# Two hypernetwork convolutions on one core: 128-column weight products, tiles in groups of two, layer 2's x loaded by ScalarE

## The chip, the core and the metric

The kernel runs on one core of one Trainium2 chip. The metric is the time of one execution in microseconds (us); the time before is 4005.55 us, the median of three runs (4001.37 to 4008.61). All arithmetic is in fp32. The engines are TensorE (PE, with its weight loads PEld shown apart), VectorE (DVE), ScalarE (ACT), GpSimd (POOL), and SyncE (SP), which here only issues DMAs.

## The reference

Two equal layers follow each other. Each normalizes x by groups of positions, makes its own convolution weights for every sample and position from z, convolves, and adds a bias and x:

```
h = relu(ln(z @ W1 + b1, g1, be1))                      # z: (32, 256, 16) -> (32, 256, 128)
w = (h @ W2 + b2).reshape(B, L, CI, CO, K)              # 64*64*3 weights for each of 32*256 (b, l)
bias = (relu(ln(z @ Wb1 + bb1)) @ Wb2 + bb2).transpose(0, 2, 1)
x_uf = jnp.stack([xp[..., i:i + L] for i in range(K)], axis=-1)
out = jnp.einsum('sbilk,bliok->sbol', x_uf, w) + bias[None]
x = x + out(_gn(x))                                     # x: (32, 32, 64, 256), 32 groups of 8 positions
```

Most of the arithmetic is h @ W2: 8192 positions, each with 128 inputs and 12288 outputs, in each layer.

## The kernel before

**Units.** A layer is cut into 32 units (8 groups of four samples, 4 quarters of the positions), and each unit into two half-units of 32 output channels. There are 128 half-units, v = 0 to 127; the first 64 are layer 1. A half-unit has two parts on TensorE. First the *weight tiles*: 12 tiles of 8 output channels, made by `make` (L615) and moved to `wall` by `take` (L626). Then the *products* (L665): `wall` against the normalized x in `xn`, added to the residual in one of the three slots of `ring`.

**A weight tile.** W2 lies in `w2` as 128 x (64 channels x 192 columns), three blocks of 64 columns per channel. `make` writes one PSUM tile `pg` of 128 x 8 x 128. For each channel it has two products of 64 stationary columns and 128 moving ones, one for the lower and one for the upper half of the partitions (L622, L623). Kind 0 takes blocks 1 and 2 with the odd positions, kind 1 blocks 0 and 1 with the even ones, and kind 2 (the shared one) block 2 with the even and block 0 with the odd ones. For kinds 0 and 1 `take` is one VectorE addition of b2 over all partitions (L634). For kind 2 VectorE adds the lower 64 partitions and then ScalarE the upper 64, by eight activations (L645), whose first waits for VectorE's addition. `pg` comes from a pool of three buffers of two PSUM banks (`ps_g`); which of them a tile gets is decided while the program is built.

**Order.** The tiles of a half-unit come in the order kind 0, 2, 1, four times. The loop at L821 writes out half-unit v as: the matmuls of its first tile, then `products(v - 1)`, then `take` of the first tile and the other tiles; behind tile k it writes the work that `agenda(v)` lists for k. That covers storing the finished half-unit, loading the next residual and bias (`after`, L725), the normalization of the next half of a unit on GpSimd (`next_half`, L694) with the load of the half after it, the bias addition on GpSimd, and in layer 1 the statistics and the *rims*: `take_edges` copies the outer columns on ScalarE behind tile 1, `turn_edges` transposes them on TensorE behind tile 3. Every engine and DMA queue works through its own list in this order.

**Loads of x.** In layer 1 half a unit is one DMA (L168) of SP's queue. In layer 2 it is four DMAs of 32 partitions in short pieces (L177), also of SP's queue, into `raw` or `land`.

**The start.** `first_phase` (L440) streams x in 22 pieces for the statistics of the first groups (L458), runs the small hypernetworks and makes the first weight tiles. Behind piece 19 it normalizes unit 0 on VectorE (`starting`, L759); behind that stand the last two pieces. The bias of half-unit 0 is loaded into `xn` behind piece 18 and added behind piece 19.

Of the kernel before, what the change touches and what calls it, by code (L numbers as in the profile page):

```python
# [30 lines left out]
P = 128  # L31
K = 3
G = 32
NT = 4
# [9 lines left out]
def conv_layers(  # L44
# [78 lines left out]
    def place_of(u):  # L123
        n, r = divmod(u, UL)
        return (n, *divmod(r, BG))
# [37 lines left out]
    def load_half(u, k, buf=None):  # L163

        buf = raw if buf is None else buf
        n, q, bg = place_of(u)
        if n == 0:
            nc.sync.dma_start(out=by_slot(buf), in_=xp[u][:, k * NT // 2 : (k + 1) * NT // 2])  # L168
            return
        if k == 0:  # L170
            load_edges(u)
        for a in range(2):
            for h in range(NH):
                rows = slice((1 - a) * C + h * CH, (1 - a) * C + (h + 1) * CH)
                src = x1[u - UL][h][k * NT // 2 * S : (k + 1) * NT // 2 * S]
                src = src.rearrange("(t s) (o a m) -> a o t s m", s=S, a=2, m=MT)[a]
                nc.sync.dma_start(out=by_sample(buf)[rows, :, :, a : a + MT], in_=src)  # L177

    def residual(v):
        return ys[:, v % RING]  # L180
# [259 lines left out]
    def first_phase(first_weights, first_bias, add_bias, starting):  # L440
# [3 lines left out]
        needed = BG * (GT + 1) // LAND  # L444
        slots = [ring[:, k * LAND * GE : (k + 1) * LAND * GE] for k in range(RING)] + [land[:, 0 : LAND * GE]]
        slots = [s.rearrange("p (k x) -> p k x", k=LAND) for s in slots]
        order = [i % 4 for i in range(needed - 2)] + [0, 1, 2, 1, 2, 1]
        assert len(order) == units

        def load(i):  # L450
# [12 lines left out]
        with tc.tile_pool(name="stage", bufs=1) as stage:  # L463
# [33 lines left out]
            def batch(j):  # L497
                return made[j] if 0 <= j < count else None

            for i in range(units):  # L500
                j, odd = divmod(i, 2)
                if batch(j - 2):
                    for k in range(2 * odd, 2 * odd + 2):
                        batch(j - 2).bias(k)
                if odd:
                    if batch(j):
                        batch(j).variance()
                    if batch(j - 1):
                        batch(j - 1).hidden(0)
                        batch(j - 1).hidden(1)  # L510
                else:
                    if batch(j):
                        batch(j).form()
                    if batch(j - 1):
                        batch(j - 1).turn()
                if i == needed:
                    merge = Merge(first_parts.rearrange("p g b f -> p g (b f)")[:, 0 : GT + 1], 0, 0)
                    table = Table(0)
                    merge.sums()
                    merge.around()  # L520
                if i == needed + 1:
                    merge.mean()
                    add_bias(0)
                    merge.root()
                    table.expand(nc.vector)
                stats(i, range(2))
                if i == needed:
                    merge.spans()
                stats(i, range(2, LAND))
                if odd and batch(j):  # L530
                    batch(j).scale()
                if i == 3:
                    nets[1].prepare(stage)
                if i == 6:
                    for x in range(2):
                        load_hidden(x)
                if i == needed - 2:
                    load_half(0, 1, land)
                    load_residual(0)
                if i == needed - 1:  # L540
                    load_half(0, 0)
                    load_w2(0, CH, C)
                if i == needed:
                    first_bias()
                if i == needed + 1:
                    table.lay(table.spread(), [nc.vector.tensor_copy, nc.scalar.copy])
                    starting()
                first_weights(i - (needed - 11))
            load_residual(1)

    with tc.manual_schedule():
        bts = {}
# [62 lines left out]
        def make(h, kind, o0):  # L615
            pg = ps_g.tile([P, OG, M], FP, tag="pg", name="pg")
            even, odd = h[:, 0, :], h[:, 1, :]

            (k0, h0), (k1, h1) = (((1, odd), (2, odd)), ((0, even), (1, even)), ((2, even), (0, odd)))[kind]
            for k in range(OG):  # L620
                w = w2[:, o0 + k, :]
                nc.tensor.matmul(pg[0:C, k, :], w[:, k0 * C : (k0 + 1) * C], h0, start=True, stop=True)  # L622
                nc.tensor.matmul(pg[C:P, k, :], w[:, k1 * C : (k1 + 1) * C], h1, start=True, stop=True)  # L623
            return pg

        def take(pg, n, kind, o0):  # L626
# [64 lines left out]
        def place_half(u, k):  # L691
            return land if k == 1 and u >= 3 * BG else raw

        def next_half(u, k):  # L694

            if u >= U:
                return
            if k == 0 and u % BG == 0 and u // BG in tables:
                t = tables.pop(u // BG)
                t.lay(t.from_spot(), [nc.gpsimd.tensor_copy])  # L700
            normalize(u, k, place_half(u, k))
            u, k = (u, 1) if k == 0 else (u + 1, 0)
            if u < U:
                load_half(u, k, place_half(u, k))

        pieces = [(j, bg, g) for j in range(1, NQ) for g in range(FIRST[j]) for bg in range(BG)]
        base = BG * FIRST[0]
# [17 lines left out]
        def after(v):  # L725

            u, h = divmod(v, NH)
            store(v)
            load_pieces(v + 1)
            if v + 2 < NH * U:  # L730
                load_residual(v + 2)
                load_bias(v + 2)
            if h == 1 and u % 2 == 1 and u + 3 < U:
                load_hidden((u + 3) // 2)

        starts = range(0, CH, OG)
        order = [(kind, o) for o in starts for kind in (0, 2, 1)]

        def weights(v, k, between=None):
            u, h = divmod(v, NH)  # L740
# [25 lines left out]
                    normalize(0, k, bufs[k], nc.vector, j0, j1)  # L766
            load_half(1, 0)

        def first_bias():
            x = xn.rearrange("p n t j s -> p (n t j s)")  # L770
            h = x.shape[1] // 2
            load_bias(0, x[:, h : h + CH * LT].rearrange("p (o l) -> p o l", l=LT))

        first_phase(first_weights, first_bias, add_bias, starting)
        bp = ctx.enter_context(tc.tile_pool(name="bias", bufs=1))
        load_bias(1)
        normalize(1, 0)
        load_half(1, 1)
        add_bias(1)

        def agenda(v):

# [1 line left out]
            u, h = divmod(v - 1, NH)  # L784
            todo[0].append(lambda: last_stats(v - 1))
            todo[0].append(lambda: after(v - 1))
            todo[2].append(lambda: next_half(*((u + 1, 1) if h == 0 else (u + 2, 0))))
            if v + 1 < NH * U:
                todo[5].append(lambda: add_bias(v + 1))
            if v <= last_of[NQ - 1]:  # L790
# [24 lines left out]
            if v <= NH * UL:  # L815
                todo[1].append(lambda: take_edges(v - 1))
                if h == 1:
                    todo[3].append(lambda: turn_edges(u))
            return todo

        for v in range(1, NH * U):  # L821
# [101 lines left out]
```

## Time and profile before

| what | us |
|---|---|
| median of three runs | 4005.55 |
| the profiled execution | 4010.21 |
| its span, first to last instruction | 4008.4 |
| PE busy in the span | 3810.9 (95%) |
| DVE, ACT, POOL busy | 2592.2, 1285.8, 1939.5 |
| mean granted share of TensorE's clock | 0.986 |

The profile was taken in an execution of its own, which is 4.66 us above the median. Busy times are unions over an engine's instructions. TensorE's matmuls overlap (an fp32 product is two MATMUL rows), so its speed is read from the distances between starts.

### The profile page before, as it was taken

What the parts mean: (1) busy time and instruction counts of PE and PEld (TensorE: products, weight loads), DVE (VectorE), ACT (ScalarE), POOL (GpSimd) and SP (SyncE); (2) the same over time, 40 slices, a digit from 0 to 9 for tenths busy, and PEclk for the clock granted to TensorE, in tenths of its full rate; (3) what the DMA queues carried; (4) which work ended last, traced back from release to release, by engine and by line L of the source; (5) the groups of instructions that cost most, each with busy time, mean ns of one, the idle gap of its engine ahead of it and who ended that gap; (6) DMA issues with size and microseconds to landing.
All of it is one profiled execution on the core that took longest, in us unless ns stands there. A gap on an engine that the chain in (4) does not pass through costs nothing.

```text
span 4008.4 us, 185362 instructions
## 1 busy us (share of the span) xinstructions
PE 3810.9 (95%) x86548; PEld 3675.3 (92%) x86548; DVE 2592.2 (65%) x2954; ACT 1285.8 (32%) x4431; POOL 1939.5 (48%) x655
## 2 busy tenths in 40 slices
PE   6699999999999999999999999999999999999999
PEld 3499999999999999999989999999999999999998
DVE  4677777777777776666665555555555555555655
ACT  3423333323333333333323323323233233333332
POOL 2154445444544445544545545555546545645551
PEclk7799999999999999999999999999999999999999
DMA  8666556556556555445488878878788788788782
GB/s 271 233 201 195 180 177 193 177 172 195 177 178 196 173 168 159 134 153 156 134 196 154 148 132 160 145 147 151 140 166 141 140 156 141 147 150 140 157 146 87
DMA packets 644660, 657.76 MB, mean 164 GB/s; under 512 B 562600, under 2 KB 570160, under 8 KB 578096
## 3 DMA queue, kind: packets, MB, share of 16 engines
q1 hardware_dynamic: 624688, 633.30, 65.5%
q8 instruction: 677, 11.09, 1.2%
q10 hardware_dynamic: 19200, 12.59, 1.0%
q14 instruction: 95, 0.78, 0.1%
HBM read 496.91 MB, written 148.90 MB: 161 GB/s over the span
## 4 chain that ended last, share of the span: by engine, by line
PE 80%; DVE 6%; ACT 6%; issue 2%; DMA 1%; POOL 0%; SPq 0%; ACTq 0%; POOLq 0%; DVEq 0%
PE pg L622 49%; PE pc L676 24%; PE pg L623 6%; ACT wall L645 5%; DVE wall L634 4%; DMA bt<-bd 1%; DVE ring L685 1%; DVE parts L341 0%; POOL ring L566 0%; DVE xn L608 0%; PE pe L586 0%; DVE first_parts L723 0%; ACT rim L581 0%; PE over L371 0%; SPq L559 0%
## 5 line engine op out<-in xcount | busy, mean ns | idle before, releaser
L622 PE MATMUL pg<-hT,w2t 128*64 128x128 f32 x24576 | 2752.5, 274 | 26.7 <-issue 24.0
L623 PE MATMUL pg<-hT,w2t 128*64 128x128 f32 x24576 | 2753.3, 274 | 17.0 <-issue 16.7
L622 PEld LDWEIGHTS pg<-hT,w2t 128*64 128x64 f32 x24576 | 2689.0, 137 | 63.9 <-issue 37.9
L623 PEld LDWEIGHTS pg<-hT,w2t 128*64 128x64 f32 x24576 | 2689.2, 137 | 23.1 <-issue 22.7
L634 DVE TENSOR_TENSOR wall<-pg,b 128x1024 f32<-128x1024 f32 (+1 forms) x1536 | 1874.1, 1220 | 726.0 <-PE pg L623 720.1
L645 ACT ACTIVATE wall<-pg,b 64x128 f32<-64x128 f32 x4096 | 1158.8, 465 | 2596.1 <-DVE wall L634 2596.0
L566 POOL TENSOR_TENSOR ring<-ring,bt 128x2048 f32<-128x2048 f32 x127 | 578.1, 4552 | 1200.9 <-DMA bt<-bd 755.1
L676 PEld LDWEIGHTS pc<-wall,xn 128*32 128x32 f32 x36864 | 914.8, 110 | 110.3 <-issue 61.2
L676 PE MATMUL pc<-wall,xn 128*32 128x128 f32 (+1 forms) x36864 | 951.6, 262 | 64.1 <-issue 34.7
L685 DVE TENSOR_TENSOR ring<-pc,ring 128x512 f32<-128x512 f32 x512 | 353.9, 691 | 622.2 <-PE pc L676 617.9
L608 POOL TENSOR_TENSOR xn<-raw,tab 128x2112 f32<-128x2112 f32 x86 | 440.1, 5118 | 447.2 <-PE pc L676 433.7
L608 POOL TENSOR_TENSOR xn<-xn,tab 128x2112 f32<-128x2112 f32 x126 | 591.4, 4693 | 9.9
L608 POOL TENSOR_TENSOR xn<-land,tab 128x2112 f32<-128x2112 f32 x40 | 224.3, 5609 | 111.9 <-DMA land<-x 102.0
L341 DVE BATCH_NORM_STATS2 parts<-ring 128x6 f32<-128x256 f32 x512 | 192.1, 417 | 6.5
L723 DVE BATCH_NORM_STATS2 first_parts<-land 128x6 f32<-128x512 f32 x168 | 114.5, 681 | 0.6 <-DMA land<-in_xg_dram 0.6
L433 POOL COPY tab<-spot 64x1024 f32<-64x1024 f32 x28 | 29.0, 1035 | 94.1 <-ACT spot L420 93.2
L276 POOL TENSOR_TENSOR raw<-w2t,xn 128x256 f32<-128x256 f32 x16 | 10.3, 644 | 113.7 <-DVE xn L271 113.7
L300 PE MATMUL ph<-xn,wc 17*128 17x512 f32 x128 | 34.7, 771 | 26.7 <-DVE xn L266 15.3
L458 DVE BATCH_NORM_STATS2 first_parts<-ring 128x6 f32<-128x512 f32 x72 | 44.2, 676 | 17.3 <-DMA ring<-in_xg_dram 17.3
L300 PEld LDWEIGHTS ph<-xn,wc 17*128 17x128 f32 x128 | 10.0, 214 | 44.2 <-DVE xn L266 19.5
L302 ACT ACTIVATE xn<-ph,vec 128x1024 f32<-128x1024 f32 x32 | 37.5, 1198 | 9.8 <-ACT xn L302 5.7
L586 PEld LDWEIGHTS pe<-ident,rim 128*128 128x128 f32 x32 | 4.5, 139 | 36.0 <-ACT rim L581 36.0
(87 smaller groups left out, 368.8 us busy)
## 6 DMA issues: line engine op xcount, KB each, us to landing
bt<-bd SPq DMA_DIRECT2D x508, 256.0 KB, 10.6
ring<-in_xs_dram SPq DMA_DIRECT2D x64, 1024.0 KB, 11.1
x<-ring SPq DMA_DIRECT2D x64, 1024.0 KB, 4.9
ring<-x SPq DMA_DIRECT2D x64, 1024.0 KB, 9.5
out_dram<-ring SPq DMA_DIRECT2D x64, 1024.0 KB, 4.8
raw<-in_xp_dram SPq DMA_DIRECT2D x55, 1056.0 KB, 14.6
land<-in_xg_dram SPq DMA_DIRECT2D x46, 1024.0 KB, 8.2
raw<-x SPq DMA_DIRECT2D x128, 256.0 KB, 7.7
```

The lines of the kernel that those rows point to most:

```text
L300: nc.tensor.matmul(p[:, r], self.w.wc[x, net], self.zq[x, net], start=True, stop=True)
L341: nc.vector.bn_stats(out, y.rearrange("p o (a m) -> p o a m", a=2)[:, :, :, g * e : (g + 1) * e])
L458: nc.vector.bn_stats(first_parts[:, g, bg], slots[order[i]][:, k])
L566: nc.gpsimd.tensor_tensor(y, y, bts.pop(v), ALU.add)
L608: eng.tensor_tensor(o, i, tab[:, x, None, j0:j1].to_broadcast(list(o.shape)), op)
L622: nc.tensor.matmul(pg[0:C, k, :], w[:, k0 * C : (k0 + 1) * C], h0, start=True, stop=True)
L623: nc.tensor.matmul(pg[C:P, k, :], w[:, k1 * C : (k1 + 1) * C], h1, start=True, stop=True)
L634: nc.vector.tensor_tensor(place(rows, a), pg[rows].rearrange("p o (t m) -> p t m o", t=NT), b2[n][rows, kind, None, None, o0 : o0 + OG].to ...
L645: nc.scalar.activation(place(rows, a)[:, :, :, k], pg[rows, k].rearrange("p (t m) -> p t m", t=NT), AF.Identity, bias=b2[n][rows, kind, o0 ...
L676: nc.tensor.matmul(pc[t * S : (t + 1) * S, n0 - q * EB : n1 - q * EB, :], xn[:, u % 2, t, p, :], wall[:, t, a : a + (n1 - n0) * CH], start ...
L685: nc.vector.tensor_tensor(part, pc.rearrange("p (m a) o -> p o a m", a=2), part, ALU.add)
L723: nc.vector.bn_stats(first_parts[:, g, bg], lands[i % LAND])
```

## The change

The two products of a channel become one of 128 stationary columns where their blocks lie side by side (kinds 0 and 1); kind 2 stays as it was. The tiles are put in the order 0, 0, 2, 2, 1, 1, twice. In layer 2 the four DMAs that load half a unit are issued by ScalarE, behind each kind-2 tile. The transpose of the rims moves from behind tile 3 to behind tile 7. In the start, the first bias gets a place in `w2` and is loaded and added earlier, and the statistics of the last two pieces move into half-unit 1, with the loads that depend on them.

```
     def load_half(u, k, buf=None):
...
+        nc.sync.dma_start(out=by_slot(buf), in_=xp[u][:, k * NT // 2 : (k + 1) * NT // 2])
+    def parts_of_half(u, k, buf):
+        def part(a, h):
...
+            nc.scalar.dma_start(out=by_sample(buf)[rows, :, :, a : a + MT], in_=src)
+        return [lambda a=a, h=h: part(a, h) for a in range(2) for h in range(NH)]
...
-        order = [i % 4 for i in range(needed - 2)] + [0, 1, 2, 1, 2, 1]
+        order = [i % 4 for i in range(needed - 2)] + [1, 2, 1, 2, 1, 2]
...
-            for i in range(units):
+            for i in range(needed + 2):
...
-                    add_bias(0)
...
+                if i == needed // 2:
+                    first_bias(half_w2[:, 0 : CH * LT])
+                if i == needed - 6:
+                    load_residual(0)
+                if i == needed - 3:
+                    add_bias(0)
...
+        rest = [lambda i=i, k=k: stats(i, range(k, k + 2)) for i in range(needed + 2, units) for k in (0, 2)]
...
-            (k0, h0), (k1, h1) = (((1, odd), (2, odd)), ((0, even), (1, even)), ((2, even), (0, odd)))[kind]
             for k in range(OG):
                 w = w2[:, o0 + k, :]
-                nc.tensor.matmul(pg[0:C, k, :], w[:, k0 * C : (k0 + 1) * C], h0, start=True, stop=True)
-                nc.tensor.matmul(pg[C:P, k, :], w[:, k1 * C : (k1 + 1) * C], h1, start=True, stop=True)
+                if kind < 2:
+                    cols = slice((1 - kind) * C, (3 - kind) * C)
+                    nc.tensor.matmul(pg[:, k, :], w[:, cols], (odd, even)[kind], start=True, stop=True)
+                else:
+                    nc.tensor.matmul(pg[0:C, k, :], w[:, 2 * C :], even, start=True, stop=True)
+                    nc.tensor.matmul(pg[C:P, k, :], w[:, 0:C], odd, start=True, stop=True)
...
-        order = [(kind, o) for o in starts for kind in (0, 2, 1)]
+        order = [(kind, o + x) for o in starts[::2] for kind in (0, 2, 1) for x in (0, OG)]
...
+            if v == 1:
+                for i, f in enumerate(rest):
+                    todo[1 + i].append(f)
+                todo[2].append(lambda: load_residual(1))
+                todo[2].append(lambda: add_bias(1))
...
+            x, k = half_after(*half)
+            if UL <= x < U:
+                at_once = [i for i, (kind, _) in enumerate(order) if kind == 2]
+                for i, part in zip(at_once, parts_of_half(x, k, place_half(x, k))):
+                    todo[i].append(part)
...
-                    todo[3].append(lambda: turn_edges(u))
+                    todo[7].append(lambda: turn_edges(u))
```

**TensorE's list in layer 2.** Before, this is where the tenth, eleventh and twelfth tile of half-unit 80 begin; each `pg` with its own number is a tile, and the bracket names the engine whose semaphore its first product waits for:

```order
L622 MATMUL pg_35538<-hT_33671,w2t_184 64x128 [waits DVE_49]
L623 MATMUL pg_35538<-hT_33671,w2t_184 64x128
...
L622 MATMUL pg_35556<-hT_33671,w2t_184 64x128 [waits DVE_49]
L623 MATMUL pg_35556<-hT_33671,w2t_184 64x128
...
L622 MATMUL pg_35582<-hT_33671,w2t_184 64x128 [waits Activation_49]
L623 MATMUL pg_35582<-hT_33671,w2t_184 64x128
```

In the changed program the same place of half-unit 81, its eleventh and twelfth tile, the first tile of half-unit 82 and the products behind that, reads:

```order
L625 MATMUL pg_30751<-hT_28799,w2t_184 128x128 [waits Activation_49]
L625 MATMUL pg_30751<-hT_28799,w2t_184 128x128 x7
L625 MATMUL pg_30761<-hT_28799,w2t_184 128x128 [waits DVE_49]
L625 MATMUL pg_30761<-hT_28799,w2t_184 128x128 x7
L625 MATMUL pg_30771<-hT_28799,w2t_184 128x128 [waits DVE_49]
L625 MATMUL pg_30771<-hT_28799,w2t_184 128x128 x7
L681 MATMUL pc_30780<-wall_189,xn_185 32x64 [waits Activation_49]
```

The names do not show where a tile lies. In the built program before, a `pg` tile gets a buffer that was last used two, three or four tiles earlier, and a kind-2 tile's buffer is used again four tiles later (three tiles of the start aside). In the changed program pg_30751, pg_30761 and pg_30771 lie in the same buffer: the wait of pg_30761 is for the addition that reads pg_30751, the tile just before it, and that of pg_30771 for the addition that reads pg_30761. This is so at the twelfth tile and at the first tile of the next half-unit from half-unit 61 to 125, 126 times in all. In layer 1 it is not; there, and in layer 2 too, the sixth tile has the buffer of the third (a kind-2 tile), and in layer 1 also the twelfth that of the ninth.

**ScalarE's list in layer 2.** Before, the activations of one kind-2 tile follow those of the last:

```order
L645 ACTIVATE wall<-pg,b_1_212 64x128 [waits DVE_49,Activation_49]
L645 ACTIVATE wall<-pg,b_1_212 64x128 [waits Activation_49] x7
L645 ACTIVATE wall<-pg,b_1_212 64x128 [waits DVE_49,Activation_49]
L645 ACTIVATE wall<-pg,b_1_212 64x128 [waits Activation_49] x7
L645 ACTIVATE wall<-pg,b_1_212 64x128 [waits DVE_49,Activation_49]
```

Now a DMA stands behind each group of eight, with its own waits for other DMAs (DMAHW) and for GpSimd (Pool):

```order
L650 ACTIVATE wall<-pg,b_1_212 64x128 [waits DVE_49,Activation_49]
L650 ACTIVATE wall<-pg,b_1_212 64x128 [waits Activation_49] x7
L174 DMA raw<-x_17_89 32x64x32 [waits DMAHW5_49,Pool_49]
L650 ACTIVATE wall<-pg,b_1_212 64x128 [waits DVE_49,Activation_49]
L650 ACTIVATE wall<-pg,b_1_212 64x128 [waits Activation_49] x7
L174 DMA raw<-x_17_89 32x64x32 [waits DMAHW3_49,DMAHW1_49]
```

What moved is the DMAs, from SP's list to ScalarE's, one behind each of the four kind-2 tiles.

**VectorE's list at the start**, from the last of the normalization of unit 0 (L608, now L611) to the first products (L685, now L690). Before:

```order
L608 TENSOR_TENSOR xn<-land,tab 128x2x256
L608 TENSOR_TENSOR xn<-xn,tab 128x2x256
L458 BN_STATS first_parts<-ring 128x6 x8
L685 TENSOR_TENSOR ring<-pc,ring 128x64x8
L341 BN_STATS parts<-ring 128x6 x2
```

Now:

```order
L611 TENSOR_TENSOR xn<-land,tab 128x2x256
L611 TENSOR_TENSOR xn<-xn,tab 128x2x256
L690 TENSOR_TENSOR ring<-pc,ring 128x64x8
L340 BN_STATS parts<-ring 128x6 x2
```

The eight statistics in front of the first products are gone; they now stand in twos between the additions of half-unit 1.

## Rows read from the trace of the kernel before

**Rows 1.** The page: span, busy times, and the chain that ended last.
```profile
span 4008.4 us, 185362 instructions
...
PE 3810.9 (95%) x86548; PEld 3675.3 (92%) x86548; DVE 2592.2 (65%) x2954; ACT 1285.8 (32%) x4431; POOL 1939.5 (48%) x655
...
PE 80%; DVE 6%; ACT 6%; issue 2%; DMA 1%; POOL 0%; SPq 0%; ACTq 0%; POOLq 0%; DVEq 0%
```

**Rows 2.** Waits of TensorE: who waited for what, us in total, times, longest.
```profile
PE pc L676 <- issue: 34.7, 87, 3.1
PE pe L586 <- ACT rim L581: 28.3, 32, 1.0
PE pg L622 <- issue: 24.0, 27, 2.3
PE pg L623 <- issue: 16.7, 21, 2.3
...
PE pc L676 <- ACT wall L645: 12.1, 61, 1.9
```

**Rows 3.** The same for the weight loads.
```profile
PEld pg L622 <- issue: 37.9, 56, 2.5
PEld pe L586 <- ACT rim L581: 36.0, 32, 1.3
PEld pc L676 <- ACT wall L645: 28.4, 66, 2.2
PEld pg L623 <- issue: 22.7, 26, 2.5
```

**Rows 4.** Timeline, layer 2, end of a weight tile: start, length, engine, line.
```profile
2619.41 0.27 PE L622 MATMUL pg<-hT,w2t 128*64 128x128 f32 x1
...
2619.42 0.27 PE L623 MATMUL pg<-hT,w2t 128*64 128x128 f32 x1
...
2619.52 0.27 PE L622 MATMUL pg<-hT,w2t 128*64 128x128 f32 x1
...
2619.74 1.22 DVE L634 TENSOR_TENSOR wall<-pg,b 64x1024 f32<-64x1024 f32 x1 [0.52 <-PE pg L623]
```

**Rows 5.** Timeline of VectorE in the same half-unit.
```profile
2617.99 1.22 DVE L634 TENSOR_TENSOR wall<-pg,b 128x1024 f32<-128x1024 f32 x1 [0.52 <-PE pg L623]
...
2621.48 1.23 DVE L634 TENSOR_TENSOR wall<-pg,b 128x1024 f32<-128x1024 f32 x1 [0.53 <-PE pg L623]
```

**Rows 6.** Timeline of ScalarE in the same half-unit.
```profile
2621.05 2.26 ACT L645 ACTIVATE wall<-pg,b 64x128 f32<-64x128 f32 x8 [2.96 <-DVE wall L634]
```

**Rows 7.** Timeline around a transpose of the rims.
```profile
242.08 0.30 ACT L581 COPY rim<-ring 128x64 f32<-128x64 f32 x1
...
242.43 0.33 PE L586 MATMUL pe<-ident,rim 128*128 128x128 f32 x1 [1.02 <-ACT rim L581]
242.69 0.32 PE L622 MATMUL pg<-hT,w2t 128*64 128x128 f32 x1
```

**Rows 8.** Timeline of the start: products of 128 stationary, 136 moving columns; weight loads.
```profile
126.45 1.19 PE L248 MATMUL pt<-form,w2t 128*128 128x136 f32 x8
...
126.45 0.99 PEld L248 LDWEIGHTS pt<-form,w2t 128*128 128x128 f32 x8 [0.39 <-PE pb L318]
```

**Rows 9.** Stretches: us, busy by engine, granted clock, DMA share, GB/s.
```profile
126.40:127.70 1.30, 1.30 (x12) 1.25 (x11) 1.30 (x3) 0.69 (x2) 0.00 (x0) 1.00 0.97 396
2101.00:2121.00 20.00, 17.78 (x272) 16.72 (x272) 12.71 (x16) 10.09 (x40) 14.00 (x4) 0.91 0.96 201
2157.10:3966.90 1809.80, 1756.91 (x41004) 1718.19 (x41004) 1057.35 (x976) 554.66 (x1958) 954.98 (x330) 1.00 0.78 146
```

**Rows 10.** The chain in order of time, at the start.
```profile
180.08 0.76 DVE xn L608
181.05 4.77 DVE xn L608
...
194.69 4.84 DVE first_parts L458 x8
```

**Rows 11.** Timeline of GpSimd and SP at the start, and VectorE in the second products.
```profile
180.18 5.01 POOL L566 TENSOR_TENSOR ring<-ring,xn 128x2048 f32<-128x2048 f32 x1 [40.78 <-ACT tab L435]
...
215.16 4.68 POOL L608 TENSOR_TENSOR xn<-raw,tab 128x2112 f32<-128x2112 f32 x1
...
199.55 0.33 SPq L184 DMA_DIRECT2D ring<-in_xs_dram  x1
...
230.50 0.69 DVE L685 TENSOR_TENSOR ring<-pc,ring 128x512 f32<-128x512 f32 x1 [2.09 <-PE pc L676]
```

**Rows 12.** Line 177: SP's time for one issue, ns min/median/max, first and last start.
```profile
L177 SPq DMA_DIRECT2D land<-x x128: 422/2006/10742, 2038.9 to 3903.4; - x128
```

**Rows 13.** The page's DMA issues: count, size, median us to landing.
```profile
ring<-in_xs_dram SPq DMA_DIRECT2D x64, 1024.0 KB, 11.1
```

More of the change, by code (lines that the diff above doesn't have):

```diff
@@ L165, in load_half @@
         buf = raw if buf is None else buf
[L166 to L177, printed above, removed]
+        nc.sync.dma_start(out=by_slot(buf), in_=xp[u][:, k * NT // 2 : (k + 1) * NT // 2])
+    def parts_of_half(u, k, buf):
+        def part(a, h):
+            rows = slice((1 - a) * C + h * CH, (1 - a) * C + (h + 1) * CH)
+            src = x1[u - UL][h][k * NT // 2 * S : (k + 1) * NT // 2 * S]
+            src = src.rearrange("(t s) (o a m) -> a o t s m", s=S, a=2, m=MT)[a]
+            nc.scalar.dma_start(out=by_sample(buf)[rows, :, :, a : a + MT], in_=src)
+        return [lambda a=a, h=h: part(a, h) for a in range(2) for h in range(NH)]
     def residual(v):
@@ L536, in first_phase @@
                         load_hidden(x)
+                if i == needed // 2:
[4 more added lines that the diff above has]
+                    add_bias(0)
                 if i == needed - 2:
                     load_half(0, 1, land)
-                    load_residual(0)
                 if i == needed - 1:
@@ L542, in first_phase @@
                     load_w2(0, CH, C)
-                if i == needed:
-                    first_bias()
                 if i == needed + 1:
@@ L548, in first_phase @@
                 first_weights(i - (needed - 11))
-            load_residual(1)
+        rest = [lambda i=i, k=k: stats(i, range(k, k + 2)) for i in range(needed + 2, units) for k in (0, 2)]
+        assert len(rest) == 2 * (RING - 1)
+        return rest
     with tc.manual_schedule():
@@ L701, in next_half, with half_after @@
             normalize(u, k, place_half(u, k))
-            u, k = (u, 1) if k == 0 else (u + 1, 0)
-            if u < U:
+            u, k = half_after(u, k)
+            if u < UL:
                 load_half(u, k, place_half(u, k))
+            elif u < U and k == 0:
+                load_edges(u)
+        def half_after(u, k):
+            return (u, 1) if k == 0 else (u + 1, 0)
         pieces = [(j, bg, g) for j in range(1, NQ) for g in range(FIRST[j]) for bg in range(BG)]
@@ L729, in after @@
             load_pieces(v + 1)
-            if v + 2 < NH * U:
+            if 0 < v < NH * U - 2:
                 load_residual(v + 2)
@@ L767, in starting, with first_bias @@
             load_half(1, 0)
[L769 to L774, printed above, removed]
+        def first_bias(buf):
+            load_bias(0, buf.rearrange("p (o l) -> p o l", l=LT))
+        rest = first_phase(first_weights, first_bias, add_bias, starting)
         bp = ctx.enter_context(tc.tile_pool(name="bias", bufs=1))
@@ L778, in conv_layers @@
         load_half(1, 1)
-        add_bias(1)
         def agenda(v):
@@ L786, in agenda @@
             todo[0].append(lambda: after(v - 1))
-            todo[2].append(lambda: next_half(*((u + 1, 1) if h == 0 else (u + 2, 0))))
+            half = (u + 1, 1) if h == 0 else (u + 2, 0)
+            todo[2].append(lambda: next_half(*half))
+            if v == 1:
[3 more added lines that the diff above has]
+                todo[2].append(lambda: add_bias(1))
+                todo[4].append(lambda: load_residual(2))
+                todo[4].append(lambda: load_bias(2))
+            x, k = half_after(*half)
[3 more added lines that the diff above has]
+                    todo[i].append(part)
             if v + 1 < NH * U:
```

## The prediction

> **What bounds the kernel now.** The page comes first: of a span of 4008.4 us TensorE is busy 95%, and it holds 80% of the chain that ended last [rows 1]. So only two things change the time: how fast TensorE streams, and how long it stands still. The table of waits, for the matmuls and for the weight loads, names the standstills [rows 2, 3]. None of them is a wait of a weight tile for VectorE's or ScalarE's reading of a `pg` buffer. How near such a wait is stands in the timeline of one weight tile of layer 2 [rows 4 to 6]: its last product starts at 2619.42, the next tile begins at 2619.52, VectorE's addition begins at 2619.74 and takes 1.22, ScalarE's eight activations run from 2621.05 for 2.26. A tile takes 1.75 us (additions start at 2617.99, 2619.74, 2621.48 [rows 4, 5]). VectorE sits idle 0.52 us per tile, yet every buffer is read out late: 1.44 us (VectorE alone) or 3.8 us (ScalarE's tile) after the next tile has begun. With a buffer used again two to four tiles later nobody notices. So the change has to be judged by which buffer each tile gets.
>
> **The rate of the products: 0.** The old pair moves 128 columns through each half of the array at once; one full-width product moves the same 128 columns. In the timeline a pair follows a pair after 0.11 us (2619.41, 2619.52 [rows 4]). Full-width products with new weights each time stand in the start: eight rows take 1.19 us at granted clock 1.00 [rows 8, 9]; less the last one's own 0.28 or so that is seven steps in 0.91, 0.13 each with the first, uncovered load in it, for 136 columns. That is 0.11 to 0.12 for 128. Ends: a gain of 0, since the columns are the same; a loss of 0.005 us on each of the 16,384 new rows (8 tiles of 8 products of two rows, 128 times), 82 us. I take 0, as the single uncovered load explains nearly all of the difference.
>
> *A rule against it.* The Trainium skill, "TensorE: Matmul & The Clock Gate", Part 3, "The mechanism", says that weight loads overlap running matmuls only where the row groups differ. All loads here take all 128 rows, so by it each full-width load would lie open. The eight loads of [rows 8] are busy 0.99 us, 0.12 each, beside eight matmuls that need 1.19 in all: they overlap, and the rule does not hold for this stream. By the rule the sum would grow by 16,384 x 0.12, about 2.0 ms, to some 6.1 ms (a rival below).
>
> **A tile that takes the buffer of the tile before it: +195.** In 126 places of layer 2 (last tile of a half-unit, first tile of the next) the first product waits for the addition that reads the tile just made. In the timeline that would be: last product 2619.42, addition 2619.74 to 2620.96, then TensorE. From an engine's end to TensorE's start I use the rims: copy ends at 242.38, transpose starts at 242.43, 0.05 [rows 7]. So TensorE starts at 2621.01 where it would have started at 2619.52: 1.49. Starting again costs a little (after the transpose the second weight pair follows later than 0.11); with 0.06 for it, 1.55 x 126 = 195. Ends: 1.22 (the addition alone), 154; 1.75 (a whole tile's time), 220. Nothing covers it: TensorE works in order, and the addition cannot begin before the tile's last product.
>
> **Two shared tiles in a row: +74.** The third tile's buffer (kind 2) is wanted by the sixth tile, and in layer 1 the ninth's by the twelfth. By [rows 4, 6] ScalarE is done at 2623.31, so TensorE may start at 2623.36; two tiles in between end the sixth tile's turn at 2619.52 + 2 x 1.745 = 2623.01. That is 0.35, with the restart 0.40. About 61 half-units with two such places and 63 with one make 185: 74. Ends: 0 (ScalarE a third of a microsecond sooner) and 110 (0.6 each, where statistics push VectorE back in layer 1).
>
> **What the change removes.** The wait for the rims: 28.3 by the matmuls, 36.0 by the loads [rows 2, 3]; behind tile 7 the copy is four tiles older, so all of it: -33. The wait of the products for ScalarE's last tile: 12.1 to 28.4 [rows 2, 3]; the last kind-2 tile is now the tenth, so -20. "Issue", where TensorE waits for nothing that is shown: 24.0 and 16.7 on the pairs by the matmuls, 60.6 by the loads [rows 2, 3], against 34.7 on the products. I read it as TensorE's instruction list running dry: the pairs start four rows (two loads, two matmuls) per 0.11 us, full-width products two. Two thirds of the tiles halve their rows, and the new waits let the list fill: -38 of about 50. Ends 0 and -60. The products keep theirs.
>
> **ScalarE's DMAs: 0, with a wide end.** Four issues per half-unit go from SP, where one takes 2.0 us in the median and up to 10.7 [rows 12], to ScalarE, behind its activations, and each also waits for older DMAs. Behind the first of a pair stands the second kind-2 tile. The tight place is the tenth tile, whose activations the products need: tenth tile's last product to the products is a tile of 1.75, a wait, a tile, a wait, a tile, 8.3 us; the ninth tile's activations end 2.15 us into this (3.9 less a tile of 1.75), its DMA takes t, the tenth's take 2.26. So t up to 3.9 us costs nothing, and each microsecond more costs 63 (once per half-unit). SP's list gets shorter; nobody on the path waits for it. I take 0, since the median lies below 3.9.
>
> **The start: -9, and +6 in half-unit 1.** The eight statistics in front of the first products, 4.84 us on the chain, move [rows 10]. One normalization step took 4.77 instead of 0.76 [rows 10] while GpSimd added the bias from 180.18 to 185.19 [rows 11]; that addition now comes earlier: -4.0. Against it the residual of half-unit 1 was requested at 199.55; now the request stands behind the statistics and behind a load that needs GpSimd to have begun the half at 215.16 [rows 11]. Some 218 plus 11.1 for landing [rows 13] plus 4.6 for the addition on GpSimd is 234. The first addition of the second products came at 230.50, and two PSUM buffers let TensorE go on for about 2 us more: a stall of 0 to 12, taken as 6. The first bias itself is hidden behind the hypernetworks.
>
> **Sum.** 195 + 74 - 33 - 20 - 38 - 9 + 6 = +175. On the profiled execution's 4010.2 that is 4185; this execution lay 4.7 above the median, so 4180, 4.4% slower.
>
> **Rivals.**
> *The reading-out keeps ahead (faster).* If the tiles found free buffers, as they do now, only the gains are left: -33 - 20 - 38 - 9 + 6 = -94, 3912. For it speaks that VectorE is idle 0.52 us per tile. Against it: that idle time lies before the addition, not behind it. It decides where a wait in the 126 places is worth less than (94 - 74) / 126 = 0.16 us, and the addition alone takes 1.22.
> *ScalarE's DMAs block (slower still).* If an issue on ScalarE, with its waits, takes 5 to 7 us, the tenth tile is late by 1 to 3: 63 to 190 more, 4240 to 4370. For it speaks the maximum of 10.7 [rows 12]; against it that SP issued four at a time and ScalarE spreads them over a half-unit.
> *The clock falls.* After the long standstill of the layer change the granted clock is 0.91 in a stretch [rows 9]. If the new waits held all of layer 2 there, its 1757 us of matmul time would grow by 9%, 158: 4340. The Trainium skill, same page, "A second HAM failure mode: psum-queue depth-cycling", warns of such pauses between groups of matmuls. But layer 2 now contains pauses of up to 2.3 us [rows 2] and has 1.00 [rows 9].
> *Open loads,* as above: 6.1 ms.
> *Nothing happens:* the waits happen to pay for the gains; that needs the 126 waits near 0.16 us.
>
> **Chances and range.** The forecast 0.80, with its own range 4110 to 4250 from the ends (waits 154 to 220 and 0 to 110, issue 0 to -60). ScalarE blocking 0.10, faster 0.05, clock 0.02, open loads 0.01, no change 0.02. From 4100 to 4260 holds 8 in 10. About 0.2% is what a measurement of this kernel can tell from no change: faster 0.05, same 0.02, slower 0.93.
>
> **What the new profile would show.** TensorE's table of waits gets two new rows, a weight tile behind VectorE's `wall`, about 126 times and 1.5 us each, in layer 2 alone, and one behind ScalarE's `wall`, some 185 times. The rims and the products' wait for ScalarE are gone, "issue" on weight tiles is down to a fourth. Full-width rows follow each other after 0.11. A half-unit of layer 2 lasts about 32.5 us where it lasted 29.7 (1809.8 us over 61 [rows 9]); layer 1 keeps its pace. The prediction is wrong if the two waits are missing, if ScalarE's DMAs stand in front of a late tenth tile, or if the full-width rows are further apart than the pairs.

## The result and the profile after

The changed kernel takes 4221.59 us (median of four runs, 4216.04 to 4222.76) against 4003.46 (four runs, 4000.03 to 4008.61): 1.054 of the time before, 95% interval 1.0523 to 1.0559, 218 us slower. The forecast was 4180 and the range 4100 to 4260. The profiled execution took 4216.04; its span is 206 us longer than that of [rows 1].

The page of the changed kernel, span and busy times, shows fewer matmul rows and a span that grew all the same; the granted share of the clock is 0.988.

```profile
span 4214.3 us, 152947 instructions
...
PE 3960.0 (94%) x70164; PEld 3752.1 (89%) x70164; DVE 2591.9 (62%) x2954; ACT 1231.9 (29%) x4431; POOL 1935.1 (46%) x655
```

The table of TensorE's waits, matmuls first and then weight loads (who waited for what, us in total, times, longest):

```profile
PE pg L625 <- DVE wall L639: 169.4, 131, 1.3
...
PE pc L681 <- issue: 9.8, 14, 3.0
...
PE pg L625 <- issue: 1.5, 2, 1.2
...
PE pg L625 <- ACT wall L650: 1.3, 5, 0.3
...
PEld pg L625 <- DVE wall L639: 194.7, 133, 1.5
PEld pg L625 <- issue: 44.7, 253, 1.3
```

Against [rows 2, 3]: the rims are gone, the products' wait for ScalarE is gone, and "issue" of the matmuls fell from 34.7 + 24.0 + 16.7 = 75 to 11. In their place stands one row of the matmuls, a weight tile behind VectorE's `wall`. The weight loads have a second new one: before 253 loads of full-width products they stand still for 0.18 us on average, with nothing named. The other forecast row, behind ScalarE's `wall`, has 5 entries and not 185.

The stretches say where it happens (columns as in [rows 9]): layer 1 without its ends, layer 2 without its start, and the last half-unit of it.

```profile
252.20:2001.60 1749.40, 1742.87 (x31642) 1673.55 (x31641) 1267.93 (x1582) 544.57 (x2036) 831.25 (x231) 1.00 0.55 170
2175.00:4171.90 1996.90, 1840.15 (x33197) 1757.27 (x33196) 1057.27 (x976) 527.42 (x1958) 952.01 (x330) 1.00 0.71 132
4142.20:4171.90 29.70, 29.70 (x545) 28.67 (x544) 17.33 (x16) 8.59 (x32) 4.54 (x1) 1.00 0.37 108
```

The 61 half-units of layer 2 take 32.7 us each, where [rows 9] have 29.7. The clock is 1.00 in the whole layer, pauses and all. The last half-unit, for which no x is left to load and whose tiles do not get the buffer of the tile before, takes 29.7 in the same execution. That is a first comparison, though not a clean one, since this half-unit differs in both respects. The 58 half-units of layer 1 take 30.2, where the same ones (products from 260.2 to 1997.2) take 29.9 in the kernel before.

One half-unit of layer 2 in the timeline (start, length, engine, line), rows of TensorE (one of its weight loads among them), ScalarE and VectorE together, with most rows left out:

```profile
3201.51 0.61 PE L625 MATMUL pg<-hT,w2t 128*128 128x128 f32 x4
3202.05 0.32 PE L627 MATMUL pg<-hT,w2t 128*64 128x128 f32 x1
...
3202.21 0.27 PE L627 MATMUL pg<-hT,w2t 128*64 128x128 f32 x1
...
3205.49 0.27 PE L628 MATMUL pg<-hT,w2t 128*64 128x128 f32 x1
3205.66 1.97 ACT L650 ACTIVATE wall<-pg,b 64x128 f32<-64x128 f32 x7
3205.70 0.60 PE L625 MATMUL pg<-hT,w2t 128*128 128x128 f32 x3
...
3207.25 0.93 PE L625 MATMUL pg<-hT,w2t 128*128 128x128 f32 x5
...
3208.01 5.30 PE L625 MATMUL pg<-hT,w2t 128*128 128x128 f32 x46
...
3216.89 1.86 PEld L625 LDWEIGHTS pg<-hT,w2t 128*128 128x128 f32 x16 [0.17 <-issue]
3216.89 2.05 PE L625 MATMUL pg<-hT,w2t 128*128 128x128 f32 x16
...
3218.97 1.22 DVE L639 TENSOR_TENSOR wall<-pg,b 128x1024 f32<-128x1024 f32 x1 [0.76 <-PE pg L625]
...
3220.25 2.05 PE L625 MATMUL pg<-hT,w2t 128*128 128x128 f32 x16 [1.31 <-DVE wall L639]
...
3222.34 1.22 DVE L639 TENSOR_TENSOR wall<-pg,b 128x1024 f32<-128x1024 f32 x1 [2.14 <-PE pg L625]
...
3223.62 2.05 PE L625 MATMUL pg<-hT,w2t 128*128 128x128 f32 x16 [1.31 <-DVE wall L639]
```

*The long wait* is at the end: three tiles in one buffer (3216.89, 3220.25, 3223.62). The last row of the first starts at 3216.89 + 2.05 - 0.27 = 3218.67; the addition begins 0.30 later, takes 1.22, and TensorE starts 0.06 behind its end. From tile to tile it is 3.37 us, where an undisturbed tile of this kind takes 1.79. So one such place costs 1.58, and 126 of them 199.

Three things in these rows were not in the forecast, or not in this size. *The step of full-width rows,* in the run of 46: (5.30 - 0.27) / 45 = 0.1118. Over all rows of these tiles the mean is 0.1117, where the pairs' steps are 0.1092: 0.0025 more on 16,384 rows, 41 us. *The change of form.* From the last pair (3205.49) to the first full-width row it is 0.21 instead of 0.11, and the next two steps take 0.60 - 0.27 = 0.33 instead of 0.22: 0.20 lost. From the last full-width row (3201.51 + 0.61 - 0.27 = 3201.85) to the first pair it is 0.20, and the second pair comes after 0.16: 0.14 lost. A half-unit has two of each, 0.67 us with all digits, which is 85 for 127 half-units. The weight loads show what is late: behind pairs, at 3216.89, the first full-width load has stood still for 0.17 and begins together with its own row. Inside a run each load begins with the row before its own. Of the 253 places in the table 250 are such changes from pairs to full-width rows. *The sixth tile.* The five rows at 3207.25 take 0.93 - 0.27 = 0.66 for four steps of which two are late by 0.10; the tile starts at 3207.69. The last seven of ScalarE's eight activations, the row at 3205.66, end at 3205.66 + 1.97 = 3207.63. So the wait for ScalarE is there, but it costs 0.2, too short to stand in the table of waits.

### The profile page after: what moved, and what is told of

It reads as the page before. It is cut to its first block, busy times and chain, and to the rows that moved or that the text cites. A ratio compares the mean times of both kernels' runs of the same rounds, so it can differ in the third digit from the quotient of the medians.

```text
span 4214.3 us, 152947 instructions
## 1 busy us (share of the span) xinstructions
PE 3960.0 (94%) x70164; PEld 3752.1 (89%) x70164; DVE 2591.9 (62%) x2954; ACT 1231.9 (29%) x4431; POOL 1935.1 (46%) x655
## 4 chain that ended last, share of the span: by engine, by line
PE 88%; DVE 5%; ACT 1%; issue 1%; ACTq 0%
PE pg L625 45%; PE pc L681 22%; PE pg L627 20%; DVE wall L639 4%; PE pg L628 1%; ACT wall L650 1%; PE spread L415 0%; DVE first_parts L733 0%; ACT parts L362 0%; PE over L370 0%; PE pe L589 0%; ACT first_parts L362 0%; DVE apart L365 0%; ACT over L389 0%; DVE moments L390 0%
## 5 line engine op out<-in xcount | busy, mean ns | idle before, releaser
L625 PE MATMUL pg<-hT,w2t 128*128 128x128 f32 x16384 | 2016.7, 280 | 173.7 <-DVE wall L639 169.4
L625 PEld LDWEIGHTS pg<-hT,w2t 128*128 128x128 f32 x16384 | 1892.0, 192 | 283.9 <-DVE wall L639 194.7
L650 ACT ACTIVATE wall<-pg,b 64x128 f32<-64x128 f32 x4096 | 1103.7, 472 | 2045.4 <-DVE wall L639 2041.8
L681 PE MATMUL pc<-wall,xn 128*32 128x128 f32 (+1 forms) x36864 | 938.5, 262 | 18.6 <-issue 9.8
L627 PE MATMUL pg<-hT,w2t 128*64 128x128 f32 x8192 | 954.4, 275 | 1.3 <-ACT wall L650 0.7
L628 PE MATMUL pg<-hT,w2t 128*64 128x128 f32 x8192 | 954.4, 275 | 0.0
L627 PEld LDWEIGHTS pg<-hT,w2t 128*64 128x64 f32 x8192 | 890.1, 137 | 38.3 <-issue 8.4
L628 PEld LDWEIGHTS pg<-hT,w2t 128*64 128x64 f32 x8192 | 890.1, 137 | 0.0
L690 DVE TENSOR_TENSOR ring<-pc,ring 128x512 f32<-128x512 f32 x512 | 353.9, 691 | 671.1 <-PE pc L681 668.5
L611 POOL TENSOR_TENSOR xn<-raw,tab 128x2112 f32<-128x2112 f32 x86 | 438.6, 5100 | 615.2 <-PE pc L681 563.0
L611 POOL TENSOR_TENSOR xn<-xn,tab 128x2112 f32<-128x2112 f32 x126 | 591.2, 4692 | 9.9
L611 POOL TENSOR_TENSOR xn<-land,tab 128x2112 f32<-128x2112 f32 x40 | 224.0, 5601 | 124.9 <-DMA land<-x 114.6
L584 ACT COPY rim<-ring 128x64 f32<-128x64 f32 x64 | 19.4, 303 | 614.2 <-DVE ring L690 593.0
```

What stands on the lines that cost most here:

```text
L611: eng.tensor_tensor(o, i, tab[:, x, None, j0:j1].to_broadcast(list(o.shape)), op)
L625: nc.tensor.matmul(pg[:, k, :], w[:, cols], (odd, even)[kind], start=True, stop=True)
L627: nc.tensor.matmul(pg[0:C, k, :], w[:, 2 * C :], even, start=True, stop=True)
L628: nc.tensor.matmul(pg[C:P, k, :], w[:, 0:C], odd, start=True, stop=True)
L650: nc.scalar.activation(place(rows, a)[:, :, :, k], pg[rows, k].rearrange("p (t m) -> p t m", t=NT), AF.Identity, bias=b2[n][rows, kind, o0 ...
L681: nc.tensor.matmul(pc[t * S : (t + 1) * S, n0 - q * EB : n1 - q * EB, :], xn[:, u % 2, t, p, :], wall[:, t, a : a + (n1 - n0) * CH], start ...
```

## The experiments

Each ran beside the kernel before on the same chip; its ratio is to that. Distances between starts of successive matmuls, summed over the whole trace behind 240 us, stand beside the tables of waits where a stall is shorter than the tables show.

**Which part of the change makes the long wait.** One word of the changed kernel:

```
-            nc.scalar.dma_start(out=by_sample(buf)[rows, :, :, a : a + MT], in_=src)
+            nc.sync.dma_start(out=by_sample(buf)[rows, :, :, a : a + MT], in_=src)
```

> The changed kernel with one word undone: layer 2's four loads per half-unit are issued by SyncE again, at the same places of the program. In the built program the weight tiles of layer 2 then get the buffers of layer 1's pattern (reused after two to four tiles). Theory (the buffer that a tile gets is the loss): the 126 places of 1.58 us go, 199 us; the twelfth tile gets ScalarE's wait of 0.2 in 63 half-units, +13; 4222 - 199 + 13 = 4036 (4020 to 4050). Rival (VectorE and ScalarE are too slow for this order, and any rotation only moves the wait): layer 2 keeps at least half of it, above 4120.

Measured: 4041.72, ratio 1.0083 (1.0061 to 1.0106), 180 below the changed kernel. Its table of waits, and layer 2 in one stretch:

```profile
PE pg L625 <- DVE wall L639: 3.7, 5, 0.9
```

```profile
2168.40:4000.10 1831.70, 1825.83 (x33197) 1753.05 (x33196) 1057.65 (x976) 528.30 (x1958) 952.42 (x330) 1.00 0.78 144
```

The wait of 131 tiles is down to 5, and a half-unit of layer 2 takes 1831.70 / 61 = 30.0. The rival, that any rotation only moves the wait, falls.

**ScalarE's DMAs with other buffers.** The DMAs stay on ScalarE; three pools of one buffer each take the place of the pool of three, and which tile takes which is written down:

```
...
+            fixed[1] += 1
+            return fixed[0], f"pg{[1, 0, 2, 1, 0, 2, 0, 1, 2, 0, 1, 2][(fixed[1] - 1) % len([1, 0, 2, 1, 0, 2, 0, 1, 2, 0, 1, 2])]}"
...
-            pg = ps_g.tile([P, OG, M], FP, tag="pg", name="pg")
+            pool, tag = turns()
+            pg = pool.tile([P, OG, M], FP, tag=tag, name="pg")
...
+        fixed += [ctx.enter_context(tc.tile_pool(name="ps_f", bufs=1, space=PSUM)), 0]
```

> The changed kernel with ScalarE's DMAs kept, but the three buffers written down as three pools of one, turned in layer 1's pattern in every half-unit. Theory (ScalarE's DMAs cost only through the buffers): the same time as with SyncE's loads within 0.2%, about 4036. Rival (a DMA issue on ScalarE holds its activations, or the spread loads collide with others): above that by 20 us or more, the wait standing in layer 2 behind ScalarE.

Measured: 4050.60, ratio 1.0105 (1.0085 to 1.0125); the interval overlaps that of the first experiment. So it is the buffers. By the medians the DMAs on ScalarE cost 9 us, which these intervals do not tell from nothing; the time lies 15 above the expected 4036, outside its 0.2%, and short of the rival's 20. ScalarE's timeline in this kernel shows why it is so little:

```profile
3202.52 0.74 ACT L660 ACTIVATE wall<-pg,b 64x128 f32<-64x128 f32 x2 [14.24 <-DVE wall L649]
3202.82 0.31 ACTq L175 DMA_DIRECT2D land<-x  x1
3203.06 1.73 ACT L660 ACTIVATE wall<-pg,b 64x128 f32<-64x128 f32 x6
3204.55 7.94 ACTq L175 DMA_DIRECT2D land<-x  x1
3204.57 2.27 ACT L660 ACTIVATE wall<-pg,b 64x128 f32<-64x128 f32 x8
3213.72 0.48 ACT L660 ACTIVATE wall<-pg,b 64x128 f32<-64x128 f32 x1 [6.89 <-DVE wall L649]
```

One issue of a DMA takes 7.94 us, twice the 3.9 at which the prediction saw danger. The eight activations that start 0.02 us after it began do not stand behind it. In the list each DMA stands behind eight activations; the first eight are the rows of two and six from 3202.52 on, and the issue among them, at 3202.82, is theirs. The eight at 3204.57 stand ahead of the long issue, and its row begins before they have run. What stands behind it starts at 3213.72, 1.23 us after the issue's end. The changed kernel has such long issues too (ns, minimum, median, maximum; first and last start):

```profile
L174 ACTq DMA_DIRECT2D raw<-x x128: 309/310/8417, 2014.4 to 4072.4; - x128
L174 ACTq DMA_DIRECT2D land<-x x128: 309/826/9613, 2048.0 to 4105.4; - x128
```

By place in the half-unit, the 64 issues behind the fourth tile take 6.8 us in the median and up to 9.6; ScalarE's next tile comes 9.1 us after such an issue begins, in the median, and in one place alone the issue lasted until then:

```profile
3502.10 9.61 ACTq L174 DMA_DIRECT2D land<-x  x1
...
3511.82 0.48 ACT L650 ACTIVATE wall<-pg,b 64x128 f32<-64x128 f32 x1 [7.39 <-DVE wall L639]
```

The issues behind the ninth tile, where the prediction saw the tight place, take 0.31 in the median and at most 3.2, below its 3.9. Seven of these took 1.6 us or more, and in all seven ScalarE turns to the tenth tile 0.04 behind the issue's end. So an issue does hold what stands behind it; there is room for the long ones where they fall.

**What the 128-column form costs and gives.** The kernel with written-down buffers, with all products as pairs again (the removed lines of the diff put back in `make`).

> The kernel with fixed turns, and all products in pairs of 64 columns again. Theory (the 128-column form has a price and a gain of its own that nearly cancel): rows back from 0.1117 to 0.1092 us, -41; no changes between the two forms, 0.7 us per half-unit, -91; TensorE's 'issue' back, +85; the sixth and twelfth tile wait 0.4 instead of 0.2 us for ScalarE, since TensorE comes to them sooner, +50; about 4039 (4010 to 4070). Rival (the standstills called 'issue' went because of the new waits and not because of the fewer rows): they stay away, about 3955. Rival (the 0.1 us behind a change of form comes from waits for semaphores and not from the form): the pairs save only the rate, about 4130.

Measured: 4012.04, ratio 1.0013 (1.0002 to 1.0025), 39 below the full-width form: at the low edge of what the theory gave, between it and the first rival; the second rival, 4130, falls. Its table:

```profile
PE pg L634 <- ACT wall L657: 36.9, 196, 1.0
PE pc L688 <- issue: 22.3, 40, 3.6
...
PE pg L634 <- issue: 12.9, 18, 1.9
PE pg L635 <- issue: 10.3, 14, 1.7
```

"Issue" came back, but to 45.5 by the table (51 by distances), not to the 75 (96 by distances) of the kernel before. So both have a part. Fewer rows take most of it away by themselves: in the next experiment, with the old order, the table has 10.7 + 2.1 = 13. The waits that this order brings seem to take a part as well, as 45 against 75 with the old rows says; this kernel differs from the one before in more than the order. The wait for ScalarE stands in the table now that the tiles come to it sooner: by distances 68 us in 194 places, 0.35 each, which is the size the prediction worked out.

**The 128-column form alone.** The kernel before with the new `make` and nothing else.

> The kernel before with the 128-column products alone: order, loads, rims and start as before, buffers reused after two to four tiles. Between the two forms TensorE now changes eight times per half-unit instead of four. Theory (the wide form costs 0.0025 us on each of 16,384 rows and 0.67/4 = 0.17 us at each change of form): +41 and +170; 'issue' falls by 75 to 85, and the products find ScalarE's last tile done, -25; 4005 + 41 + 170 - 80 - 25 = 4111 (4080 to 4140). Rival (what stood behind the changes of form in the kernel with groups of two came from its waits for ScalarE and not from the form): 4005 + 41 - 80 - 25 = 3941, faster than before.

Measured: 4079.88, ratio 1.0177 (1.0158 to 1.0196): the bottom of the theory's range and 140 above the rival, which falls. The theory had a change too many: between the first tile of a half-unit and the second, a shared one, stand the products, so there are seven changes from one form straight to the other and not eight. That explains some 21 of the 31 us by which the theory was too high. Its trace has each at the same size: at the changes to full-width rows 0.203 and then 0.213 us from start to start, back again 0.205 and 0.153.

**No change of form at all.** On the first experiment's kernel, with the shared tiles made by one full-width product per channel too, which leaves out the values of one of the two positions:

```
-                if kind < 2:
-                    cols = slice((1 - kind) * C, (3 - kind) * C)
...
+                cols = slice((1 - kind % 2) * C, (3 - kind % 2) * C)
+                nc.tensor.matmul(pg[:, k, :], w[:, cols], (odd, even)[kind % 2], start=True, stop=True)
```

> The changed kernel with SyncE's loads (first experiment), and the shared tiles computed by one 128-column product per channel as well, which leaves out the second position's values: the output is not the reference's, and its time is read for TensorE's sake alone. No change of form is left among the weight tiles. Theory: the 0.67 us per half-unit for four changes go, -85; 8192 more rows at 0.0025 us, +20; the sixth and twelfth tile come 0.19 us sooner to ScalarE's wait, 254 x 0.19 = +48; 4042 - 85 + 20 + 48 = 4025 (4005 to 4040). Rival (the form costs nothing at its changes): 4042 + 20 = 4062 or more.

Measured: 4006.94, 35 below the first experiment's kernel. The rival falls. The time lies at the low edge of the theory's range; of the 18 by which its 4025 was too high, 10 come from the wait for ScalarE, which grew by 0.15 us at each of the 254 places and not by 0.19, and 8 stay open. In its table of the weight loads that wait now has its own row:

```profile
PEld pg L624 <- ACT wall L646: 71.8, 247, 1.5
```

**The rims alone.** The kernel before with `todo[7]` for `todo[3]` in front of `turn_edges`.

> The kernel before with one number changed: the transpose of the rims stands behind the eighth tile instead of the fourth. Theory: the 32 waits of about 1.05 us go and nothing takes their place, 4003 - 33 = 3970 (3960 to 3982), faster. Rival (the stall gives TensorE's list time to fill, and 'issue' grows by as much): 4003.

Measured: 3971.28, ratio 0.9912 (0.9891 to 0.9933). As forecast to 2 us; "issue" in its table is 30.3 + 22.9 + 14.8 = 68 and did not grow.

**What is left without the three costly parts.** The changed kernel with pairs, the old order of tiles and SyncE's loads.

> The changed kernel without its 128-column products, its groups of two and ScalarE's loads: what is left of the change is the later transpose of the rims, the start, and layer 2's loads behind each shared tile, from SyncE. Theory: -33 of the rims and -3 to -10 of the start, 4005 - 40 = 3965 (3952 to 3975). Rival (the start gives nothing by itself): as with the rims alone, 0.991 of the kernel before.

Measured: 3976.64, ratio 0.9920 (0.9897 to 0.9943), just above the theory's range; the rival holds. It is not distinguishable from the rims alone: the new start gives nothing that can be seen.

**The last wait.** The same, and

```
-        order = [(kind, o) for o in starts for kind in (0, 2, 1)]
+        order = [(kind, o) for o in starts for kind in ((0, 2, 1) if o < starts[-1] else (2, 0, 1))]
```

> The same with the last group of three tiles in the order shared, 0, 1 instead of 0, shared, 1. Theory: the products' wait for ScalarE's last tile (0.22 us in nearly every half-unit, about 28 us by the distances between starts) goes, and nothing takes its place, since in the built program the shared tiles' buffers are used again after four tiles as before: 28 below the kernel with the old order, about 3940. Rival (the shared tile that now comes two tiles after another one, not three, is late for a buffer): no gain.

Measured: 3962.99, ratio 0.9885 (0.9861 to 0.9909). The products' wait for ScalarE, which had a row of 12.6 us in 59 places in the last experiment's kernel, is gone from its table; the gain is 14 by the medians and 22 by the profiled spans. That is half to four fifths of the 28. The two ratios' intervals overlap; the next experiment, against the rims alone, differs by the same line, and there they do not.

**Two lines.** The kernel before with the rims behind the eighth tile and the last group turned round, nothing else.

> The kernel before with two lines changed: the transpose of the rims behind the eighth tile, and the last group of three tiles as shared, 0, 1. Nothing else of the change. Theory (these two waits are what can be had, and the start and SyncE's loads behind the shared tiles give nothing): 4005 - 33 - 23 = 3949 (3935 to 3965), at or below the last kernel with the new start. Rival (the new start is worth some 8 us): above that kernel's 0.9885 of the time before.

Measured: 3956.97 (six runs), ratio 0.9865 (0.9844 to 0.9886), within the theory's range and the lowest ratio of this study, though not told apart from that of the kernel before this one. The new start is not needed for it. What remains in its table is "issue", which no kernel here removes at no price:

```profile
PE pc L676 <- issue: 32.8, 64, 2.7
PE pg L623 <- issue: 21.9, 26, 2.8
PE pg L622 <- issue: 19.2, 29, 1.4
```

## Why the prediction was right

Its main step was the right one and nearly exact; several smaller ones were off, and their errors partly cancelled. That the time came out inside the range is in part luck. Of the prediction's own signs of being wrong one came true: the full-width rows are further apart than the pairs. Layer 1, which was to keep its pace, lost 0.2 us in each half-unit. Point by point, forecast and measured:

- *A tile that takes the buffer of the tile before it:* +195 forecast, 126 x 1.58 = 199 measured. Its parts were the parts seen: 0.30 to the addition, 1.22, 0.06. The two kernels with other buffers removed it, 180 and 171 us by the medians (the twelfth tile then waits for ScalarE in layer 2 too, some 13).
- *Two shared tiles in a row:* +74 forecast. In the changed kernel 185 x 0.2 = 38. The 0.35 was right for pairs (the experiment with pairs shows it); with full-width tiles TensorE comes some 0.25 us later to the place, through the slower rows and the change of form in front of it, and waits 0.1, with 0.1 for starting again.
- *The rate:* 0 was wrong, inside its bounds of 0 and 0.005 us per row. The row step is 0.0025 longer, +41. The rows of the start do not show this. Taken one by one, the first step of [rows 8] is 0.22 and the others 0.116, which scaled to 128 columns is 0.109, the pairs' step. The transposes behind them (below), 128 stationary and 128 moving columns with a load each, follow after 0.109 too. So the form alone does not make rows slower. The loads of those transposes take 0.141 in the median and those of the weight tiles 0.192; whether that is the reason no run shows.
- *Changes of form:* not in the sum at all. Going from pairs to full-width rows and back loses 0.34 us, twice in a half-unit: +85. The prediction used a stream of one form [rows 8] for a kernel that mixes two. The price stood in the trace of the kernel before (below). Inside a run the loads are hidden, as the prediction argued against the Trainium skill's rule ("TensorE: Matmul & The Clock Gate", Part 3, "The mechanism"), and the 2.0 ms did not come; the argument passed over the ends of a run.
- *"Issue":* -38 forecast, with the products keeping theirs. It fell from 96 to 11 by distances, -85. The products lost theirs too (34.7 to 9.8 in the tables, and 10.7 with the 128-column form alone). That fewer rows in the tiles leave more of the list filled when the products begin is a reading; no run shows the list.
- *The rims* -33: as forecast; alone they bring 36 by the medians. *The products' wait for ScalarE* -20 forecast, -28 by distances, for the prediction counted the places in the table and left out the short ones.
- *ScalarE's DMAs:* 0 was right, and so was the reason, though not for every issue: it allowed 3.9 us behind the ninth tile, and the longest there took 3.2. Issues of up to 9.6 us occur behind the fourth tile, which the prediction did not look at; ScalarE's next tile comes late enough there. The rival's 5 to 7 us came true in the wrong place.
- *The start:* -9 + 6 forecast. In the profiled execution the third products start 8 us sooner (252.2 for 260.2), but of the other kernels those with the new start begin them at 255.8 to 259.5 us, and those with the old one at 258.0 to 259.5. It is worth 0 to 3. Of the stall of 0 to 12 in half-unit 1 little is seen: its products take 8.93 instead of 7.14.
- *The rivals:* the clock stayed at 1.00, so that one is out. The reading-out that keeps ahead is what happens with other buffers, but even then the changed kernel is 0.8% slower than before, not 2.3% faster: the rows' step, the changes of form and ScalarE's wait eat the gains.

The price of a change of form could have been read in the trace of the kernel before, at the start, where full-width transposes end and pairs begin:

```profile
127.37 0.91 PEld L285 LDWEIGHTS pz<-ident,raw 128*128 128x128 f32 x8
127.48 1.04 PE L285 MATMUL pz<-ident,raw 128*128 128x128 f32 x8
128.45 0.13 PEld L622 LDWEIGHTS pg<-hT,w2t 128*64 128x64 f32 x1 [0.17 <-issue]
128.45 0.32 PE L622 MATMUL pg<-hT,w2t 128*64 128x128 f32 x1
```

The last transpose starts at 127.48 + 1.04 - 0.27 = 128.25 and the first pair 0.20 later; its load starts with it, after 0.17 of standing still, where the first load of the transposes began 0.11 ahead of its row. What holds the load back at a change the rows do not show.

The sum with the measured terms: 199 + 38 + 41 + 85 - 33 - 28 - 85 - 8 = 209, against 206 between the two profiled spans. The forecast of +175 was low because 126 us of costs of the full-width form (41 and 85) were missing; against them ScalarE's wait was 36 smaller, "issue" gave 47 more, the products' wait and the start 13 more, and the long wait was 4 larger. By the medians the loss is 218: the profiled execution of the changed kernel lay 5.6 below its median, that of the kernel before 6.7 above.

Why the program builder gives layer 2's tiles these buffers when ScalarE has the DMAs, and layer 1's pattern when SyncE has them, stays open; that it does is read in the two built programs, which differ in that one word.

## What to carry to other kernels

When two engines read out what a third one makes, look up in the built program which buffer each tile gets before you cost anything else: a DMA moved to another engine can change it, and one reuse of the buffer just filled costs the whole latency of reading it out (here 1.6 us), however idle the reader is. Cost a mixture of matmul forms by the changes between them, not by a stream of one. And of a change with many parts, try the smallest alone: two lines, the rims and the last group, gave 1.3% where the whole cost 5.4%.

## What the runs showed of the hardware that was not expected

- In fp32, the weight tiles' products of 128 stationary columns follow each other after 0.1117 us per row, pairs of 64 columns after 0.1092 per pair of rows, both with new weights each time at a granted clock of 1.00. Transposes of 128 stationary and 128 moving columns follow after 0.109 in the kernel before, at 1.00 too.
- A change between these two forms costs 0.20 us in one direction and 0.14 in the other, spread over the first two steps (kernels with seven, four and no changes in a half-unit). At 250 changes to full-width rows the weight loads stand still for 0.17 and then begin with their own row.
- A full-width product that just has to wait costs a second 0.10 at its next row, beside the wait.
- ScalarE's issue of a DMA in short pieces took up to 9.6 us in the changed kernel. The activations that run beside it are those ahead of it in the list; in all 256 issues nothing behind one began before its end.
